# A conv and gate kernel in two layers: when the neural-CA loads are asked for, the row length of their scratch, and the order of the sync queue

## The chip, the cores and the metric

The kernel runs on one core of a Trainium2 chip. The metric is the device time of one execution in microseconds (us). Three runs of the kernel before gave 13310.97, 13316.33 and 13325.59 us; their median, 13316.33 us, is the time before.

## What is computed

The input is 32 images of 8 channels and 256 x 256 pixels. Layer 0 works on the group-normalised image and adds its result to the image; layer 1 normalises that sum and adds a quantised 3 x 3 convolution of it. The change touches layer 0 only:

```python
xn = gn(x)
grid = drive = xn                                   # "lattice" (CML)
for _ in range(15):
    mapped = 3.9 * grid * (1.0 - grid)
    physics = 0.7 * mapped + 0.3 * conv3x3_per_channel(mapped, K_local)
    grid = 0.85 * physics + 0.15 * drive
cml = clip(grid, 0.0001, 0.9999)
nca = sigmoid(conv1x1(relu(conv3x3(xn, Wp) + bp), Wu) + bu)      # 8 -> 128 -> 8 channels
gin = concat([xn, cml, nca])                         # 24 channels
g = sigmoid(conv1x1(relu(conv3x3(gin, Wg1) + bg1), Wg2) + bg2)
out0 = x + g * cml + (1 - g) * nca
```

## The kernel before

Everything that the stages of layer 0 hand on to each other goes through scratch in DRAM. `gs_s` holds three planes of an image: the normalised input, the lattice's result and the NCA's result. `xp_s` holds the normalised input once more, split in a high and a low part for the NCA's matmuls, as `[268 rows, 2 parts, 8 channels, 258 columns]`: a row has a zero column at either end, so that a 3 x 3 window can slide over it. `y_s` holds what layer 1 reads.

Five pieces of work are written into one program for TensorE (PE):

- **prep** (`normalise`, from L293): for an image and a channel pair it loads `xr`, takes the statistics (VectorE, and two tiny matmuls), normalises in place, and makes `xq` (ScalarE, L366), `hi` (VectorE, L372) and `lo` (POOL, L373). `hi` and `lo` are tiles of 258 columns of which 256 are written. `stores` (L332, L342) sends them to `gs_s` and `xp_s`.
- **lattice** (L392): a unit is one channel of four images; there are 64 units. A unit runs 15 steps of two halves `s`, so there are 1920 halves. A half is 32 matmul instructions from L499 and three `mark` matmuls (L274), which read one of the formats `m_a` or `m_b`; VectorE then adds the drive (L510) and writes the mapped grid into the other format (L520). Every half that ends in `m_a`, except in a unit's last step, is followed by `exchange` (L474, L475): two DMAs of 33 KB from SBUF to SBUF that copy border rows between neighbouring strips. There are 896 such pairs. The `m_a` that they complete is read by the next half of the same `s`, two halves later. From step 7 on the drives of the next unit are loaded (`d_a`, then `d_b` from `d_a`), and after the last step the results are stored: `background` (L462) issues four of these small DMAs after each half.
- **nca** (L576): an image has eight tiles `t` of 32 rows. A tile is loaded into `im` by the four DMAs of `rows` (L561, the DMA is L566; two buffers). It is worked through in four pieces `i` of two `hidden` calls each (12 matmuls from L585 and a ReLU on ScalarE, L593) and a `drain` (eight matmuls, L601). The result of a tile is stored at L632, in the third piece of the tile after it.
- **gate** (L705): an image has eight tiles. `stage` (L656) loads a tile's `gin` by six DMAs (L663; two buffers for each) and `mix` by two (L672; one buffer). The 240 matmul instructions of L759 make the hidden layer, those of L715 the gate. What VectorE, ScalarE and POOL do afterwards is cut into `chores`: `mix_`, `arrange_`, `stage_`, `measured_`, `extremes_`. One chore is taken from the list at each lattice half. `arrange_` (L685 to L689) reads `mix`; `extremes_` ends in the store to `y_s` (L735).
- **layer 1** (from L911), after all of this.

`together` (L844) interleaves them by hand: after each lattice half it advances a mixture of nca, gate and prep until that has done its share by the weights that the `yield`s carry (an nca tile has 14.8 in all: 1.4 for each `hidden`, 0.9 for each `drain`).

`manual_schedule(engines={PE})` at L258 says that PE's instructions keep the order in which the program writes them. Those of the other engines, and of the sync queue (SP), which issues nearly all DMAs, are put in order by the scheduler of the compiler, by its own reckoning of when each will be ready. A DMA that has to wait for its data stands at the head of its queue meanwhile: SP stood 3264.7 us in all at L474, in 800 waits, until VectorE had written `m_a`.

In `nca` the next tile is asked for in the third piece, after both of its `hidden` calls:

```python
if i == 2:
    if done:
        nc.sync.dma_start(*done)
        done = None
    if t < NT8 - 1:
        ahead = rows(b, t + 1)
```

Of the kernel before, what the change touches and what calls it, by code (L numbers as in the profile page):

```python
# [31 lines left out]
F32 = mybir.dt.float32  # L32
# [8 lines left out]
P = 128  # L41
# [9 lines left out]
STEP = 14  # L51
PW = W + 2
PROWS = 268
ROW = 2 * C * PW
PART = PROWS * C * W
R4 = 32
NT = 9
# [52 lines left out]
def kernel(  # L110
# [48 lines left out]

    xp_s = [dp.tile([PROWS, 2, C, PW], F32, name=f"xp_s{i}") for i in range(NBUF)]
    gs_s = [dp.tile([3, PROWS, C, W], F32, name=f"gs_s{i}") for i in range(NBUF)]
    y_s = [dp.tile([PROWS, C, W], F32, name=f"y_s{b}") for b in range(B)]

    with tc.tile_pool(name="prep", bufs=1) as pp, tc.tile_pool(name="prep2", bufs=2) as pp2:
# [21 lines left out]
        G.memset(zt, 0.0)  # L188
        borders = []
        for t, at, n, w, rows in (  # L190
            *((t, 0, 2 * C, PW, ((0, 1), (257, 1))) for t in xp_s),
            *((t, j * PART, C, W, ((0, 1), (257, 1))) for t in gs_s for j in range(3)),
            *((t, 0, C, W, ((0, 1), (257, 5), (262, 5), (267, 1))) for t in y_s),
        ):
            k = 64 if w == W else 43
# [59 lines left out]
    with ExitStack() as one:  # L255


        one.enter_context(tc.manual_schedule(engines={mybir.EngineType.PE}))  # L258

        pool = lambda name, bufs, **kw: one.enter_context(  # L260
            tc.tile_pool(name=name, bufs=bufs, reuse_waits="tile", **kw)
        )
        hp, xp, sp2, gp, gip = pool("hp", 4), pool("xp", 3), pool("sp2", 1), pool("gp", 3), pool("gip", 2)
        st, imp, wk, np_ = pool("st", 2), pool("imp", 2), pool("wk", 2), pool("np", 1)
        ps_u, ps_a, ps_m = pool("ps_u", 3, space=PSUM), pool("ps_a", 1, space=PSUM), pool("ps_m", 1, space=PSUM)
        LOW, HIGH = slice(0, 64), slice(64, P)

# [6 lines left out]
            T.matmul(one_[HIGH], qw[HIGH, 0, HIGH], qw[HIGH, 0, 0:1], start=True, stop=True)  # L274

        fixed = lambda shape, name, dt=F32: np_.tile(shape, dt, name=name)
        hi, lo = fixed([P, 2, 2, PW], "hi", F32R), fixed([P, 2, 2, PW], "lo", F32R)
        for t in (hi, lo):
            for w in (0, PW - 1):
                G.memset(t[:, :, :, w].bitcast(F32), 0.0)  # L280
        TU = 2 * NT
# [11 lines left out]
        def normalise(jobs):  # L293
# [36 lines left out]
            def stores(b, g, xq):  # L330
                for h in range(2):
                    nc.sync.dma_start(  # L332
                        dram_ap(
                            gs_s[b % NBUF],
                            ((1 + P * h) * C + 2 * g) * W,
                            [[C * W, P], [W, 2], [1, W]],
                        ),
                        xq[:, :, h].rearrange("p c q j -> p c (q j)"),
                    )
                for h in range(2):  # L340
                    for j, src in enumerate((hi, lo)):
                        nc.sync.dma_start(  # L342
                            dram_ap(
                                xp_s[b % NBUF],
                                (1 + P * h) * ROW + (C * j + 2 * g) * PW,
                                [[ROW, P], [PW, 2], [1, PW]],
                            ),
                            src.bitcast(F32)[:, :, h, :],
                        )
                ready.add((b, g))  # L350

            def end(b, gs, xrs, e):
                n = len(gs)
                pv = unit()[:, 0, :]
                T.matmul(pv[:, 0:n], avg, e, start=True, stop=True)
                rstd = rstd_x[:, b, gs[0] : gs[0] + n]
                V.tensor_scalar(rstd, pv[:, 0:n], GN_EPS, None, ALU.add)
                G.tensor_tensor(rstd, rstd, mhalf[:, 0:n], ALU.pow)
                for g, xr in zip(gs, xrs):
                    flat = xr.rearrange("p c h w -> p (c h w)")  # L360
                    V.tensor_scalar(
                        flat, flat, mean_x[:, b, g : g + 1], rstd_x[:, b, g : g + 1],
                        ALU.subtract, ALU.mult,
                    )
                    xq = sp2.tile([P, 2, 2, 4, NJ], F32, name="xq", tag="xq")
                    S.activation(  # L366
                        xq.rearrange("p c h q j -> p (c h) q j"),
                        xr.rearrange("p c h (j q) -> p (c h) q j", q=4),
                        AF.Copy,
                    )  # L370
                    inner = lambda t: t[:, :, :, 1 : 1 + W]
                    V.tensor_copy(inner(hi), xr)  # L372
                    G.tensor_tensor(inner(lo), xr, inner(hi).bitcast(F32), ALU.subtract)  # L373
                    yield 0.05
                    stores(b, g, xq)
                    yield 0.05
# [15 lines left out]
        def lattice(g):  # L392
# [76 lines left out]
            def exchange(t):  # L469
# [4 lines left out]
                nc.sync.dma_start(t[0::16, :, below], t[14::16, :, above])  # L474
                nc.sync.dma_start(t[15::16, :, above], t[1::16, :, below])  # L475

            JOBS = ((0, 5), (5, 10), (10, 14), (14, 18))
            HALVES = ((slice(0, 10), 5), (slice(10, 18), 4))

            def half(c, step, s, d, m_a, m_b):  # L480
# [42 lines left out]
                if a2b:  # L523
                    edge = m_b[:, :, 0 : NJ + 1 : NJ]
                    G.tensor_tensor(edge, edge, junk.unsqueeze(1).to_broadcast([P, TU, 2]), ALU.mult)  # L525
                else:
                    exchange(m_a)
                return a2b

            if g == 0:  # L530
# [5 lines left out]
            for c in range(C):  # L536
                u = g * C + c
                for step in range(STEPS):
                    if step == 7 and u + 1 < NG * C:
                        units[u + 1], dmas = load(u + 1)  # L540
                        later.extend(dmas)
                    if step == STEPS - 1:
                        background(len(later))
                    for s in range(2):
                        d = units[u][s][1 if (step + s) % 2 == 0 else 0]
                        a2b = half(c, step, s, d, m_a[s], m_b[s])
                        if step == STEPS - 1:
# [5 lines left out]
                        yield 2.05  # L553

            stored[g] = issued[0] + len(later)
            if g == NG - 1:
                background(len(later))
# [2 lines left out]

        def rows(b, t):  # L561

            im = imp.tile([P, 2, 8, PW], F32R, name="im", tag="im")
            for k in range(2):
                for q in range(2):
                    nc.sync.dma_start(  # L566
                        im.bitcast(F32)[64 * q : 64 * q + 48, k],
                        dram_ap(
                            xp_s[b % NBUF], (32 * t + 16 * k + 8 * q) * ROW, [[PW, 48], [ROW, 8], [1, PW]]
                        ),  # L570
                    )
            return im
# [3 lines left out]
        def nca(b):  # L576
# [45 lines left out]
            for t in range(NT8):  # L622
                im = ahead
                acc = ps_a.tile([P, 512], F32, name="acc", tag="acc")
                for i in range(4):
                    hs = {}
                    for n in (i, i + 4):
                        hs[n], hs[n + 8] = hidden([im[64 * q : 64 * q + 48, :, n, :] for q in range(2)])
                        yield 1.4
                    if i == 2:  # L630
                        if done:
                            nc.sync.dma_start(*done)  # L632
                            done = None
                        if t < NT8 - 1:
                            ahead = rows(b, t + 1)
                        elif all((b + 1, g) in ready for g in range(4)):
                            loaded[b + 1] = rows(b + 1, 0)
                    if pend:
                        done = drain() or done
                    pend = (acc, t, i, hs)  # L640
# [12 lines left out]
            V.reciprocal(sc[:, 2:3], sc[:, 1:2])  # L653
            return sc

        def stage(b, t):  # L656

            src = gs_s[b % NBUF]
            gin = []
            for j in range(3):  # L660
                t_ = gip.tile([P, 4, W], F32, name=f"gin{j}", tag=f"gin{j}")
                for h in range(2):
# [4 lines left out]
                        ),  # L667
                    )
                gin.append(t_)
            mix = gip.tile([P, 3, 2, W], F32, name="mix", tag="mix", bufs=1)  # L670
            for k in range(2):
                nc.sync.dma_start(  # L672
                    mix[:, :, k, :],
                    dram_ap(src, (32 * t + 16 * k + 1) * C * W, [[W, P], [PART, 3], [1, W]]),
                )
            return gin, mix

        flat = lambda t: t.rearrange("p k w -> p (k w)")

# [12 lines left out]
        staged = {}  # L692

        def begin_gate(b):
            return scales(b), stage(b, 0)

        PARTS = (
            (1, slice(0, 256), slice(0, 256)),
# [6 lines left out]
        def gate(b):  # L705
# [39 lines left out]
            for t in range(NT8 + 1):  # L745
# [30 lines left out]
                def arrange_(now):  # L776
                    now["df"] = arrange(sc, now["mix"])

                def stage_(now):
                    if now["t"] < NT8 - 1:  # L780
                        now["ahead"] = stage(b, now["t"] + 1)
                    elif (b + 1) % GB:
                        staged[b + 1] = begin_gate(b + 1)

                def measured_(now):
                    measured(now["was"]["t"], now["was"]["y"])
# [16 lines left out]
                while t < NT8 - 1 and "ahead" not in now and chores:  # L803
                    chores.pop(0)()
                ahead = now.get("ahead")
            while chores:
# [270 lines left out]
```

## Time and profile before

| what | value |
|---|---|
| median of three runs | 13316.33 us |
| the profiled execution | 13288.75 us |
| its span, first to last instruction | 13287.0 us |
| PE busy | 11179.9 us, 84% |
| VectorE, ScalarE, POOL busy | 7782.5, 3789.6, 1552.4 us |
| mean granted TensorE clock | 0.913 |
| DMA moved | 1769.32 MB, mean 133 GB/s |
| packets of the sync and the ScalarE queue's DMAs | 58.7% and 2.2% of 16 engines' span |

The profile names each group of instructions by its line in the kernel, its engine and the tiles that it writes and reads. "Idle before" is the time that an engine stood still just before an instruction, put down to what released it. A window of the profile gives the busy time of each engine in that stretch, with the granted share of TensorE's clock (PEclk) and the share of time in which the 16 DMA engines were busy.

### The profile page before, as it was taken

What the parts mean: (1) busy time and instruction counts of PE and PEld (TensorE: products, weight loads), DVE (VectorE), ACT (ScalarE), POOL (GpSimd) and SP (SyncE); (2) the same over time, 40 slices, a digit from 0 to 9 for tenths busy, and PEclk for the clock granted to TensorE, in tenths of its full rate; (3) what the DMA queues carried; (4) which work ended last, traced back from release to release, by engine and by line L of the source; (5) the groups of instructions that cost most, each with busy time, mean ns of one, the idle gap of its engine ahead of it and who ended that gap; (6) DMA issues with size and microseconds to landing.
All of it is one profiled execution on the core that took longest, in us unless ns stands there. A gap on an engine that the chain in (4) does not pass through costs nothing. (4 is left out here: it accounts for less than half of the span.)

```text
span 13287.0 us, 372338 instructions
## 1 busy us (share of the span) xinstructions
PE 11179.9 (84%) x165152; PEld 6938.4 (52%) x165152; DVE 7782.5 (59%) x11376; ACT 3789.6 (29%) x4034; POOL 1552.4 (12%) x2242
## 2 busy tenths in 40 slices
PE   4888888888888888888888888888888989889754
PEld 2555555555555555555555555555555555555532
DVE  4555555555555565555555556555655655556477
ACT  2222222222222222222222222222222222222233
POOL 1000011111111111111111111111111110001200
PEclk7999999999999999999999999999999999999877
DMA  6554566565666656665665666656666565555778
GB/s 164 94 102 95 102 134 129 123 132 127 135 127 130 134 128 126 130 136 122 132 132 123 134 135 130 127 127 132 128 132 133 127 127 116 113 109 123 179 242 257
DMA packets 2486569, 1769.32 MB, mean 133 GB/s; under 512 B 1034336, under 2 KB 2456032, under 8 KB 2484832
## 3 DMA queue, kind: packets, MB, share of 16 engines
q1 hardware_dynamic: 2392416, 1655.96, 58.7%
q10 hardware_dynamic: 92544, 89.54, 2.2%
q8 instruction: 1299, 21.28, 0.7%
q14 instruction: 310, 2.54, 0.1%
HBM read 1133.84 MB, written 474.94 MB: 121 GB/s over the span
## 5 line engine op out<-in xcount | busy, mean ns | idle before, releaser
L593 ACT ACTIVATE h<-pt,bp_sb 128x1024 f32<-128x1024 f32 x2048 | 2273.9, 1112 | 5982.6 <-PE pt L585 5978.3
L585 PE MATMUL pt<-im,wp_hi 48*128 48x512 f32 x12288 | 2869.3, 440 | 942.8 <-DMA im<-xp_s 769.3
L510 DVE SCALAR_TENSOR_TENSOR gt<-pt,d_b 128x650 f32<-128x650 f32 (+1 forms) x1920 | 1463.8, 763 | 2432.7 <-PE mark L274 1389.4
L499 PE MATMUL pt<-m_a,lw 64*64 64x325 f32 (+1 forms) x30720 | 2464.9, 439 | 354.9 <-DMA m_a<-m_a 223.6
L585 PE MATMUL pt<-im,wp_lo 48*128 48x512 f32 x12288 | 2660.7, 410 | 0.0
L510 DVE SCALAR_TENSOR_TENSOR gt<-pt,d_a 128x640 f32<-128x640 f32 (+1 forms) x1920 | 1446.8, 754 | 2013.6 <-PE mark L274 1059.9
L585 PEld LDWEIGHTS pt<-im,wp_hi 48*128 48x128 f32 x12288 | 1340.5, 194 | 2096.5 <-issue 1460.1
L499 PE MATMUL pt<-m_b,lw 64*64 64x256 f32 (+1 forms) x30720 | 2360.9, 425 | 67.6 <-DVE gt L510 38.1
L499 PEld LDWEIGHTS pt<-m_a,lw 64*64 64x64 f32 x30720 | 1462.2, 140 | 1185.8 <-issue 455.8
L499 PEld LDWEIGHTS pt<-m_b,lw 64*64 64x64 f32 x30720 | 1413.5, 136 | 881.8 <-issue 457.2
L759 PE MATMUL pt<-gin,gw 48*32 48x192 f32 (+2 forms) x61440 | 1321.0, 305 | 240.4 <-issue 228.7
L759 PEld LDWEIGHTS pt<-gin,gw 48*32 48x32 f32 x61440 | 1150.2, 109 | 588.8 <-issue 367.9
L585 PEld LDWEIGHTS pt<-im,wp_lo 48*128 48x128 f32 x12288 | 1345.7, 195 | 208.0
L520 DVE SCALAR_TENSOR_TENSOR m_a<-gt 128x640 f32<-128x640 f32 (+1 forms) x1792 | 1414.3, 789 | 58.5
L520 DVE SCALAR_TENSOR_TENSOR m_b<-gt 128x650 f32<-128x650 f32 (+1 forms) x1792 | 1385.7, 774 | 103.0 <-DVE gt L510 3.7
L525 POOL TENSOR_TENSOR m_b<-m_b,junk 128x36 f32<-128x36 f32 x896 | 241.9, 270 | 8498.1 <-DVE m_b L520 5232.4
L601 PE MATMUL acc<-h,wu_z 128*32 128x512 f32 x8192 | 1106.6, 611 | 0.0
L274 PE MATMUL mark<-qw 64*64 64x1 bf16 x5760 | 953.0, 165 | 3.2 <-issue 1.9
L687 POOL TENSOR_TENSOR d<-mix 128x256 f32<-128x256 f32 x512 | 554.7, 1101 | 1580.5 <-DVE gate L723 1146.5
L274 PEld LDWEIGHTS <-qw 64*64 64x64 bf16 x5760 | 642.8, 112 | 142.1 <-issue 10.3
L986 PE MATMUL pt<-qt,qw 128*128 128x512 bf16 (+1 forms) x864 | 235.0, 434 | 238.4 <-ACT ob L991 238.4
L685 ACT ACTIVATE f<-mix,sc 128x512 f32<-128x512 f32 x256 | 208.5, 815 | 679.5 <-DVE y L724 476.4
(109 smaller groups left out, 5445.8 us busy)
## 6 DMA issues: line engine op xcount, KB each, us to landing
im<-xp_s SPq DMA_DIRECT2D x1024, 387.0 KB
gin<-gs_s SPq DMA_DIRECT2D x1536, 192.0 KB
mix<-gs_s SPq DMA_DIRECT2D x512, 384.0 KB
d_a<-gs_s SPq DMA_DIRECT2D x2048, 36.0 KB
yb<-y_s ACTq DMA_DIRECT2D x28, 2432.0 KB
xp_s<-hi SPq DMA_DIRECT2D x256, 258.0 KB
xp_s<-lo SPq DMA_DIRECT2D x256, 258.0 KB
xr<-in_x_dram SPq DMA_DIRECT2D x128, 512.0 KB
```

The lines of the kernel that those rows point to most:

```text
L274: T.matmul(one_[HIGH], qw[HIGH, 0, HIGH], qw[HIGH, 0, 0:1], start=True, stop=True)
L499: T.matmul(pt[dst], lw[src, c, w, dst], rhs[src], start=first, stop=not first)
L510: V.scalar_tensor_tensor(gt.rearrange("p (u c) -> p u c", u=2), pt[:, :, : w * n], FLOOR, d[:, ts, :].rearrange("p (u t) j -> p u (t j)", ...
L520: V.scalar_tensor_tensor(to, gt, 1.0, gt, ALU.subtract, ALU.mult)
L525: G.tensor_tensor(edge, edge, junk.unsqueeze(1).to_broadcast([P, TU, 2]), ALU.mult)
L585: T.matmul(ph[:, i, :].rearrange("p (h w) -> p h w", w=W), w[64 * i : 64 * i + 48, dx, :], rhs[:, :, dx : dx + W], start=(dx == 0 and w is ...
L593: S.activation(h.rearrange("p i c -> p (i c)"), ph.rearrange("p i c -> p (i c)"), AF.Relu, bias=bp_sb)
L601: T.matmul(acc[32 * g : 32 * g + 32], wu_z[:, 24 - 8 * i : 56 - 8 * i], hs[4 * g + i], start=(i == 0), stop=(i == 3),)
L685: S.activation(f, flat(mix[:, 0]), AF.Identity, bias=sc[:, 0:1], scale=sc[:, 2:3])
L687: G.tensor_tensor(d[:, cols], mix[:, 1, k], mix[:, 2, k], ALU.subtract)
L759: T.matmul(pa[32 * i : 32 * i + 32, h, to], gw[64 * h : 64 * h + 48, j, dx, :], gin[j][64 * h : 64 * h + 48, i, of], start=(j == 0 and n = ...
L986: T.matmul(pt[:, i:j, :], w[:, dx, :], qt[b % 2][h][:, k0 + i : k0 + j, dx : dx + W], start=(dx == 0), stop=(dx == 2),)
```

## The change

Four things are done; no arithmetic on the data changes, and the number of DMAs stays the same.

1. `xp_s`, `hi` and `lo` lose their two border columns: a row is 256 columns, 1024 bytes, in place of 258. The zero columns now stand in two fixed tiles `ims` in SBUF, set once; `rows` writes the 256 columns between them.
2. `rows` for the next tile is asked for after the first `hidden` of a tile, in place of after both of the third piece.
3. SP joins PE in `manual_schedule`: the sync queue keeps the program's order. With it `exchange` is no longer written in the half that needs it, but kept in `held` and written just before the next half, which is behind the nca, gate and prep work that follows.
4. `stage` is cut in two: `inputs_` asks for `gin` as the first of the chores, `blend_` asks for `mix` where `stage_` stood, after `arrange_`.

```diff
-ROW = 2 * C * PW
+ROW = 2 * C * W
...
-    xp_s = [dp.tile([PROWS, 2, C, PW], F32, name=f"xp_s{i}") for i in range(NBUF)]
+    xp_s = [dp.tile([PROWS, 2, C, W], F32, name=f"xp_s{i}") for i in range(NBUF)]
...
-        one.enter_context(tc.manual_schedule(engines={mybir.EngineType.PE}))
+        one.enter_context(tc.manual_schedule(engines={mybir.EngineType.PE, mybir.EngineType.SP}))
...
-        hi, lo = fixed([P, 2, 2, PW], "hi", F32R), fixed([P, 2, 2, PW], "lo", F32R)
-        for t in (hi, lo):
+        hi, lo = fixed([P, 2, 2, W], "hi", F32R), fixed([P, 2, 2, W], "lo", F32R)
+        ims = [fixed([P, 2, 8, PW], f"im{i}", F32R) for i in range(2)]
+        for t in ims:
             for w in (0, PW - 1):
                 G.memset(t[:, :, :, w].bitcast(F32), 0.0)
...
-                                (1 + P * h) * ROW + (C * j + 2 * g) * PW,
-                                [[ROW, P], [PW, 2], [1, PW]],
+                                (1 + P * h) * ROW + (C * j + 2 * g) * W,
+                                [[ROW, P], [W, 2], [1, W]],
...
-                    inner = lambda t: t[:, :, :, 1 : 1 + W]
-                    V.tensor_copy(inner(hi), xr)
-                    G.tensor_tensor(inner(lo), xr, inner(hi).bitcast(F32), ALU.subtract)
+                    V.tensor_copy(hi, xr)
+                    G.tensor_tensor(lo, xr, hi.bitcast(F32), ALU.subtract)
...
+            held = []
...
                 else:
-                    exchange(m_a)
+                    held.append(m_a)
                 return a2b
...
                     for s in range(2):
+                        while held:
+                            exchange(held.pop())
                         d = units[u][s][1 if (step + s) % 2 == 0 else 0]
                         a2b = half(c, step, s, d, m_a[s], m_b[s])
...
-            im = imp.tile([P, 2, 8, PW], F32R, name="im", tag="im")
+            im = ims[(NT8 * b + t) % 2]
             for k in range(2):
                 for q in range(2):
                     nc.sync.dma_start(
-                        im.bitcast(F32)[64 * q : 64 * q + 48, k],
+                        im.bitcast(F32)[64 * q : 64 * q + 48, k, :, 1 : 1 + W],
                         dram_ap(
-                            xp_s[b % NBUF], (32 * t + 16 * k + 8 * q) * ROW, [[PW, 48], [ROW, 8], [1, PW]]
+                            xp_s[b % NBUF], (32 * t + 16 * k + 8 * q) * ROW, [[W, 48], [ROW, 8], [1, W]]
                         ),
                     )
...
                         hs[n], hs[n + 8] = hidden([im[64 * q : 64 * q + 48, :, n, :] for q in range(2)])
+                        if n == 0:
+                            if t < NT8 - 1:
+                                ahead = rows(b, t + 1)
+                            elif all((b + 1, g) in ready for g in range(4)):
+                                loaded[b + 1] = rows(b + 1, 0)
                         yield 1.4
-                    if i == 2:
-                        if done:
-                            nc.sync.dma_start(*done)
-                            done = None
-                        if t < NT8 - 1:
-                            ahead = rows(b, t + 1)
-                        elif all((b + 1, g) in ready for g in range(4)):
-                            loaded[b + 1] = rows(b + 1, 0)
+                    if i == 2 and done:
+                        nc.sync.dma_start(*done)
+                        done = None
...
-                def stage_(now):
+                def inputs_(now):
                     if now["t"] < NT8 - 1:
-                        now["ahead"] = stage(b, now["t"] + 1)
+                        now["ahead"] = [inputs(b, now["t"] + 1)]
                     elif (b + 1) % GB:
-                        staged[b + 1] = begin_gate(b + 1)
+                        staged[b + 1] = [inputs(b + 1, 0)]
+
+                def blend_(now):
+                    if now["t"] < NT8 - 1:
+                        now["ahead"].append(blend(b, now["t"] + 1))
+                    elif (b + 1) % GB:
+                        staged[b + 1] = scales(b + 1), (*staged[b + 1], blend(b + 1, 0))
...
                 steps = []
+                if t < NT8:
+                    steps.append(inputs_)
                 if last:
                     steps.append(mix_)
                 if t < NT8:
-                    steps += [arrange_, stage_]
+                    steps += [arrange_, blend_]
                 if last:
                     steps += [measured_, extremes_]
```

`inputs` and `blend` are the two parts of `stage`: the loop of six `gin` DMAs, and that of two `mix` DMAs.

More of the change, by code (lines that the diff above doesn't have):

```diff
@@ L190 @@
         for t, at, n, w, rows in (
-            *((t, 0, 2 * C, PW, ((0, 1), (257, 1))) for t in xp_s),
+            *((t, 0, 2 * C, W, ((0, 1), (257, 1))) for t in xp_s),
             *((t, j * PART, C, W, ((0, 1), (257, 1))) for t in gs_s for j in range(3)),
@@ L194 @@
         ):
-            k = 64 if w == W else 43
+            k = 64
             for row, m in rows:
@@ L263 @@
         hp, xp, sp2, gp, gip = pool("hp", 4), pool("xp", 3), pool("sp2", 1), pool("gp", 3), pool("gip", 2)
-        st, imp, wk, np_ = pool("st", 2), pool("imp", 2), pool("wk", 2), pool("np", 1)
+        st, wk, np_ = pool("st", 2), pool("wk", 2), pool("np", 1)
         ps_u, ps_a, ps_m = pool("ps_u", 3, space=PSUM), pool("ps_a", 1, space=PSUM), pool("ps_m", 1, space=PSUM)
@@ L553, in lattice @@
                         yield 2.05
+            while held:
+                exchange(held.pop())
             stored[g] = issued[0] + len(later)
@@ L654, in scales, with inputs @@
             return sc
-        def stage(b, t):
+        def inputs(b, t):
             src = gs_s[b % NBUF]
@@ L669, in stage, with blend @@
                 gin.append(t_)
+            return gin
+        def blend(b, t):
+            src = gs_s[b % NBUF]
             mix = gip.tile([P, 3, 2, W], F32, name="mix", tag="mix", bufs=1)
@@ L675, in stage @@
                 )
-            return gin, mix
+            return mix
         flat = lambda t: t.rearrange("p k w -> p (k w)")
@@ L694, in begin_gate @@
         def begin_gate(b):
-            return scales(b), stage(b, 0)
+            return scales(b), (inputs(b, 0), blend(b, 0))
         PARTS = (
@@ L802, in gate @@
                 yield 2.3 if t < NT8 else 0.9
-                while t < NT8 - 1 and "ahead" not in now and chores:
+                while t < NT8 - 1 and len(now.get("ahead", ())) < 2 and chores:
                     chores.pop(0)()
```

## The prediction

> **What bounds the kernel.** I read the page's engine rows first, then PE's waits in the long middle stage, then one stall with its windows, then what the sync queue did before it.
>
> ```profile
> PE 11179.9 (84%) x165152; PEld 6938.4 (52%) x165152; DVE 7782.5 (59%) x11376; ACT 3789.6 (29%) x4034; POOL 1552.4 (12%) x2242
> ...
> PEclk7999999999999999999999999999999999999877
> ```
>
> PE is the bound: no other engine is over 59%. Its program order is fixed by hand, so each of its idle microseconds adds to the time. Of 13287 us it is idle in 2107. Its waits between 330 and 12300 us (who waits for whom; total, times, longest):
>
> ```profile
> PE pt L585 <- DMA im<-xp_s: 744.6, 164, 13.5
> PE pt L499 <- DMA m_a<-m_a: 221.4, 79, 13.0
> PE pt L759 <- issue: 163.0, 171, 4.1
> PE pt L585 <- ACT h L593: 103.9, 87, 2.7
> PE pt L499 <- DVE gt L510: 73.3, 65, 5.8
> ```
>
> Half of all the waiting is for the NCA's tile `im`, 164 times for 256 tiles. One of them by windows (us, busy time of PE, PEld, DVE, ACT, POOL, PEclk, DMA share, GB/s):
>
> ```profile
> 7125.00:7135.60 10.60, 10.59 (x118) 5.74 (x114) 7.57 (x16) 3.34 (x3) 0.00 (x0) 1.00 0.56 131
> 7135.60:7148.00 12.40, 0.00 (x0) 0.03 (x1) 1.62 (x3) 0.00 (x0) 0.25 (x1) 0.62 1.13 208
> 7148.00:7155.60 7.60, 5.57 (x29) 3.39 (x33) 0.00 (x0) 1.11 (x1) 0.00 (x0) 0.50 1.14 160
> 7155.60:7170.00 14.40, 13.27 (x329) 8.79 (x324) 9.64 (x13) 5.35 (x7) 3.86 (x5) 1.00 0.25 56
> ```
>
> PE does nothing for 12.4 us, and for 7.6 us more it works at a clock of 0.50. The sync queue, a little earlier:
>
> ```profile
> 7129.25 2.86 SPq L663 DMA_DIRECT2D gin<-gs_s  x6
> 7132.22 1.79 SPq L672 DMA_DIRECT2D mix<-gs_s  x2
> 7134.11 0.44 SPq L632 DMA_DIRECT2D gs_s<-nca  x1
> 7134.60 3.32 SPq L566 DMA_DIRECT2D im<-xp_s  x4
> 7138.02 0.62 SPq L474 DMA_DIRECT2D m_a<-m_a  x1
> ```
>
> `im` was asked for at 7134.6, when PE was one microsecond from needing it, and behind 1.9 MB of `gin` and `mix`; with its own 1.5 MB it was usable at about 7150.7. Over all tiles, the fourth `im` DMA is issued a median of 17.0 us ahead of the tile's first matmul, and 9.0 us or less in a quarter of them. The request is late; the transfers are not too slow for the stage (DMA share 0.60).
>
> **Two rules of the Trainium skill.** "TensorE: Matmul & The Clock Gate", Part 1, says that a monitor halves PE's clock after an idle window of about 3.4 us, until PE has been busy for about as long. The windows above agree: 0.62 during the gap, 0.50 after it, 1.00 from 7155.6. So a wait costs more than its own length. "DMA: Bandwidth & Descriptors", section "How a descriptor splits into AXI transactions", says that a piece whose start isn't a multiple of 256 B needs more bus transactions than its length suggests. The packets agree as far as they can: those of 1032 B took 94.5 ns in the mean (524,288 of them), those of 1024 B 59.6 ns (809,984). In the few us after their issue `im` packets had a median of 112 ns, `gin` packets, also 48 partitions read from DRAM, 67 ns. I go by the trace for both.
>
> **The change, part by part.** The sum is made against the span, 13287.0 us; the profiled execution (13288.75) is 27.6 us under the median of the runs shown.
>
> *The earlier request.* It moves from 10.2 to 1.4 of a tile's 14.8 weights, and a tile lasts 47.6 us (median), so some 28 us are won, more where the scheduler had let it slip. The buffer allows it: tile t+1 overwrites tile t-1, whose last matmul lies before the new place. To see what the new queue order does I wrote down all SP instructions in program order with the change and laid them along the old trace: each starts when the queue is free and its producer has ended in the trace, and lasts as long as its kind did (0.4 to 0.65 us). The fourth `im` DMA then stands 33 us or more ahead of its use in 99% of tiles, with a median of 48, against a landing of some 8 to 16. So the wait goes: -740, keeping the first tile's, which has no tile ahead of it. In 28 us, some four halves, the four DMAs move past about two pairs of `exchange`, up to 17 background DMAs, a set of `gin` and `mix` and an `nca` store; that is priced below.
>
> *The clock.* By the trace's clock records 1833 us between 300 and 12700 were at half clock, in 208 stretches, and PE was busy in 1204 of them. The 12 `hidden` matmuls of L585 take 1.66 us at full and 3.2 to 5.9 at half clock, a lattice half 2.4 and 4.5, so half of the 1204, some 600 us, is loss. 115 stretches with 1191 us follow a gap at L585, 39 with 304 us one at `m_a`. The first group goes: 600 x 1191/1833 = -390. It can't be kept, unless other gaps take their place.
>
> *Rows of 1024 B.* 393,216 `im` packets and 131,072 to `xp_s`. If `im` falls from 94.5 to `gin`'s 67 ns, 393216 x 27.5 ns / 16 = 0.68 ms of each DMA engine go, out of 8.2 ms. PE does not wait for bandwidth, so directly this is 0; it shortens what an `exchange` finds ahead of it. The new pitch in SBUF (1032 B, starting 4 B in) is not shown by any load of the trace; `d_b<-d_a`, whose 256 B pieces are written at a pitch of 260 B, has the same median packet, 18 ns, as the aligned `d_a`. Bounds: 47 ns (the fastest) to 112 (nothing won). I take 67.
>
> *The queue in program order, and `exchange` behind the fill.* Now, SP stands waiting when VectorE finishes `m_a`: in 75% of cases the DMA goes out within 0.07 us, in 95% within 2.3. Laid along the trace, the new order gives 0.06 in 75% and 1.5 in 95%, since SP mostly gets through the fill's DMAs before VectorE is done. Ahead of `exchange` in its queue now stand up to four background DMAs, `im`, `gin`, `mix` and the stores, and behind their waits all SP work: 813 us of waits for the last step's clamp (L517), 169 for POOL's `f`, 126 for `y`, 135 for `d_a`. They fit: some 11,700 DMAs of about 0.55 us over 1920 halves are 3.4 us in a half of 6.4. What does not vanish is what is in the DMA rings ahead of it: an `exchange` takes 2.3 us from issue to its last packet (median), 10.1 at the 95th percentile. From issue to need there are 5.5 us (median), 4.1 in a quarter. `im`, `gin` and the stores of `prep` now come at the program's places, some just ahead of an `exchange`, and PE loses the slack that its `im` waits gave. Counting what the rings hold, wait by wait, I get 180 us with `im` packets at 47 ns, 360 at 67, 1190 at 112. Pairs behind the same load share a wait, and lost slack adds: I take 350 for 221 today, +130, and in proportion to its clock stretches (about 100 now) +60.
>
> *`gin` ahead of `mix_` and `arrange_`.* Six DMAs of 0.45 us move ahead of one or two halves' background DMAs (some 2 us each) and of one `exchange`. PE waits 11 us for `gin` today, all after 12300: 0, -10 to +10. `blend_` stays behind POOL's last read of the single `mix` buffer, so the last 430 us, where gate runs alone, keep their loop.
>
> *Small things*: two memsets of 129 ns more or fewer; `hi` (0.69 us) and `lo` (2.2 us) read without the gap, 128 each, off PE's path: 0. In the first 330 us stores can hold up the next image's load: -20 to +20, taken as 0. VectorE, ScalarE and POOL are still ordered by the scheduler and may come out differently, and with less idling PE will meet them more often (waits at `h`, `gt`, `rstd` of some 250 us now): +30.
>
> Sum: 13287 - 740 - 390 + 130 + 60 + 30 = 12377; with what lies around the span and the distance to the median (+29) 12406. I say 12420.
>
> **The rivals.**
>
> 1. *`exchange` is no later than now* (0.20). For it: smaller `im` packets, and SP that waits at `exchange` anyway. Then 12377 - 190 leaves 12187, with the 29 some 12200; if its waits shrink too, 12080.
> 2. *The rings* (0.17). If the SBUF side makes the packets dear (95 ns), `exchange` waits 790 us: +570, +200 of clock in place of 190: 12990, or 12900 with shared waits. Against it: the fast `d_b` packets.
> 3. *The queue blocks* (0.06): slower. The place is L474. In program order a store whose producer VectorE or POOL is late with stands ahead of `exchange`. There are 5.5 - 2.3 = 3.2 us to spare; all of the 1130 us gained are gone when 896 exchanges make PE wait 1.26 us each, that is from a mean lateness of about 4.5 us. At 5 us: 896 x 1.8 = 1610, so 13800. Against it: the 1.5 us above, and that SP would have to be late at every one.
> 4. *It does not do what it says* (0.03): the request is written early, but SP gets there late, and the wait stays: 13300.
>
> The forecast has 0.54, and its own range is 12200 to 12700. The range of 8 in 10 leaves out cases 3 and 4, half of 2 and the far end of 1: 12080 to 12920. Within 0.2% of 13316 (what a measurement can tell) only case 4 ends, 0.03; slower is case 3, 0.06; faster is the rest, 0.91.
>
> **What would show it.** Right: the row `pt L585 <- DMA im<-xp_s` falls under 60 us, and PEclk stands at 0.96 or more in the middle; no 1032 B packets; SP still waits for VectorE at `exchange`. The `m_a` row shows the new price: 150 to 600. Wrong would be an `im` row of some hundreds (case 4), an `m_a` row over 800 with DMA queued ahead (2), or with `exchange` issued late (3), or long waits for VectorE at L499.

## The result and the profile after

The changed kernel took 13370.76 us (median of 5; 13350.67 to 13379.49) against 13316.33 (median of 5): ratio 1.0036, 95% interval 1.0021 to 1.0051. It is slightly slower, where 12420 was forecast. The profiled execution has a span of 13348.8 us, 61.8 more than before.

The page's engine row and clock row hardly differ from those before:

```profile
PE 11191.9 (84%) x165152; PEld 6958.4 (52%) x165152; DVE 7851.3 (59%) x11376; ACT 3786.3 (28%) x4034; POOL 1574.7 (12%) x2242
...
PEclk7999999999999999999999999999999999999877
```

PE's waits between 330 and 12300 us do differ (L500, L590, L769 are what L499, L585, L759 were):

```profile
PE pt L769 <- issue: 638.2, 211, 8.8
PE pt L500 <- DMA m_a<-m_a: 549.5, 138, 10.5
PE pt L590 <- ACT h L598: 105.0, 83, 2.0
PE pt L500 <- DVE gt L511: 65.3, 80, 2.1
```

`im` is not among the long waits any more. Over the whole span the three rows were, before:

```profile
PE pt L585 <- DMA im<-xp_s: 769.3, 166, 22.6
PE pt L759 <- issue: 228.7, 208, 4.4
PE pt L499 <- DMA m_a<-m_a: 223.6, 81, 13.0
```

and are, with the change:

```profile
PE pt L769 <- issue: 709.8, 250, 8.8
PE pt L500 <- DMA m_a<-m_a: 559.7, 144, 10.5
PE pt L590 <- DMA im<-xp_s: 19.9, 2, 18.2
```

Two rows have grown in place of `im`: the gate's matmuls waiting for "issue", and the exchange. The three differences, -749.4, +481.1 and +336.1, add up to +67.8 us, and the span grew by 61.8 (PE's busy time by 12.0). So the gain was made in full and given back.

"Issue" is time in which PE waits for nothing that the profile shows. What it waits for is seen in one gate tile of the changed kernel, first by the sync queue, then by PE:

```profile
6667.53 1.93 SPq L571 DMA_DIRECT2D im<-xp_s  x4
6675.44 0.62 SPq L474 DMA_DIRECT2D m_a<-m_a  x1
6676.11 0.62 SPq L475 DMA_DIRECT2D m_a<-m_a  x1
6676.77 4.31 SPq L668 DMA_DIRECT2D gin<-gs_s  x6
```

```profile
6673.78 2.63 PE L769 MATMUL pt<-gin,gw 48*32 48x256 f32 x126
6680.99 1.60 PE L769 MATMUL pt<-gin,gw 48*32 48x63 f32 x41 [4.57 <-issue]
```

and by windows (us, PE, PEld, DVE, ACT, POOL, PEclk, DMA share, GB/s):

```profile
6674.00:6676.40 2.40, 2.40 (x126) 2.16 (x110) 2.33 (x5) 0.61 (x1) 0.30 (x1) 1.00 1.15 141
6676.40:6681.00 4.60, 0.03 (x3) 0.01 (x3) 3.56 (x9) 0.81 (x1) 3.23 (x4) 0.85 1.08 175
6681.00:6685.00 4.00, 4.00 (x118) 3.73 (x122) 0.00 (x0) 0.16 (x1) 0.00 (x0) 0.50 0.87 191
```

`im` is asked for at 6667.5, the DMA engines are full (a share of 1.08 to 1.15), PE gets through about half of the gate's 240 matmuls and 240 weight loads in 2.6 us, and then stands still for 4.6 us and goes on at half clock. The page shows a DMA queue for instructions:

```profile
q8 instruction: 1298, 21.27, 0.7%
```

These are 1298 packets of 16,384 bytes. PE's 330,304 matmuls and weight loads are 254 to a packet, so nearly all of them are PE's, at 64 bytes an instruction and 256 to a packet. In the packet records one starts at 6677.49, a microsecond after PE has stopped, and has landed at 6679.25; PE goes on 1.7 us later. It is the rule: there are 171 stalls of over 1 us inside a gate; in 145 a block lands within the stall, in the others less than 1 us before it, and they end 1.25 to 1.68 us after the last block landed (5th to 95th percentile, median 1.45). Of 234 other stalls of PE over 1 us between 330 and 12000 us only 23 end 1.2 to 1.75 us after a block, against 166 of the 171. The gate uses 480 instructions, nearly two blocks, in 4.66 us when nothing stops it. The Trainium skill, "Runtime: NRT & Kernel Launch", section "Instruction fetch mechanics", says that each engine's sequencer fetches the next 16 KiB block by a DMA queue of its own and that this is mostly hidden. Block size and queue agree with the trace; hidden it was not here, where 710 us of PE were lost in front of and inside gates.

### The profile page after: what moved, and what is told of

Its sections match the earlier page's. It is cut to its first block, busy times and chain, and to the rows that moved or that the text cites. A ratio compares the mean times of both kernels' runs of the same rounds, so it can differ in the third digit from the quotient of the medians.

```text
span 13348.8 us, 372548 instructions
## 1 busy us (share of the span) xinstructions
PE 11191.9 (84%) x165152; PEld 6958.4 (52%) x165152; DVE 7851.3 (59%) x11376; ACT 3786.3 (28%) x4034; POOL 1574.7 (12%) x2242
## 3 DMA queue, kind: packets, MB, share of 16 engines
q8 instruction: 1298, 21.27, 0.7%
## 5 line engine op out<-in xcount | busy, mean ns | idle before, releaser
L500 PE MATMUL pt<-m_a,lw 64*64 64x260 f32 (+1 forms) x30720 | 2528.3, 449 | 641.1 <-DMA m_a<-m_a 559.7
L590 PE MATMUL pt<-im,wp_hi 48*128 48x512 f32 x12288 | 2632.3, 425 | 152.0 <-ACT h L598 106.8
L500 PE MATMUL pt<-m_b,lw 64*64 64x320 f32 (+1 forms) x30720 | 2433.5, 436 | 123.9 <-DVE gt L511 61.3
L590 PE MATMUL pt<-im,wp_lo 48*128 48x512 f32 x12288 | 2442.6, 394 | 0.7 <-issue 0.7
L500 PEld LDWEIGHTS pt<-m_a,lw 64*64 64x64 f32 x30720 | 1525.8, 143 | 1470.2 <-issue 794.7
L769 PE MATMUL pt<-gin,gw 48*32 48x192 f32 (+2 forms) x61440 | 1422.0, 321 | 753.1 <-issue 709.8
L500 PEld LDWEIGHTS pt<-m_b,lw 64*64 64x64 f32 x30720 | 1444.8, 140 | 957.3 <-issue 529.7
L590 PEld LDWEIGHTS pt<-im,wp_hi 48*128 48x128 f32 x12288 | 1163.3, 186 | 1274.3 <-issue 768.9
L769 PEld LDWEIGHTS pt<-gin,gw 48*32 48x32 f32 x61440 | 1218.2, 115 | 1137.5 <-issue 872.6
L590 PEld LDWEIGHTS pt<-im,wp_lo 48*128 48x128 f32 x12288 | 1169.2, 186 | 204.4 <-issue 0.9
L777 ACT ACTIVATE r<-pt,bv 128x512 f32<-128x512 f32 x256 | 175.8, 687 | 1181.4 <-PE pt L769 1181.3
```

The costliest lines, as they stand in the source:

```text
L500: T.matmul(pt[dst], lw[src, c, w, dst], rhs[src], start=first, stop=not first)
L590: T.matmul(ph[:, i, :].rearrange("p (h w) -> p h w", w=W), w[64 * i : 64 * i + 48, dx, :], rhs[:, :, dx : dx + W], start=(dx == 0 and w is ...
L769: T.matmul(pa[32 * i : 32 * i + 32, h, to], gw[64 * h : 64 * h + 48, j, dx, :], gin[j][64 * h : 64 * h + 48, i, of], start=(j == 0 and n = ...
L777: S.activation(r1.rearrange("p (k w) -> p k w", w=W), pa[:, :, :W], AF.Relu, bias=bv[:, 0:1])
```

## The experiments

Theory 1: where `im`'s 1.5 MB stand. Moved to the first piece, they are in the DMA rings (DMAs that the queue has issued and that are not yet carried out) just when the gate needs instruction blocks, and ahead of exchanges. Theory 2: slack. A PE that doesn't wait for `im` outruns its instruction fetch and its exchange wherever `im` is asked for. Theory 3: the sync queue's program order makes the exchange late.

Ratios are to runs of the kernel before made beside each kernel, whose medians lay between 13284 and 13316 us, with their 95% intervals; kernels are compared by these ratios. Waits are PE's over the whole span of the profiled execution. An exchange can come late in two ways: *lateness* is the time from VectorE's end to its first DMA's issue; what it takes from issue to its last packet beyond the usual 2.3 us is put down to the *ring*. Each wait for `m_a` is counted under the larger of the two.

| kernel | time, us | ratio | `im` wait | gate's issue | `m_a` wait |
|---|---|---|---|---|---|
| before | 13316 | 1 | 769 | 229 | 224 |
| changed | 13371 | 1.0036 (1.0021 to 1.0051) | 20 | 710 | 560 |
| a_ask_late | 13806 | 1.0376 (1.0359 to 1.0394) | 296 | 217 | 1164 |
| a_ask_n2 | 12836 | 0.9650 (0.9631 to 0.9670) | 21 | 213 | 744 |
| a_spread | 12565 | 0.9441 (0.9422 to 0.9460) | 21 | 393 | 328 |
| a_im_eighth | 12004 | 0.9020 (0.9003 to 0.9037) | 11 | 217 | 163 |
| b_early | 13117 | 0.9875 (0.9853 to 0.9898) | 24 | 746 | 308 |
| b_rows | 13257 | 0.9976 (0.9967 to 0.9985) | 738 | 225 | 212 |
| a_sched_sp | 13036 | 0.9818 (0.9793 to 0.9843) | 20 | 714 | 311 |
| a_gin_late | 13484 | 1.0157 (1.0134 to 1.0180) | 21 | 625 | 823 |
| no_held | 13475 | 1.0147 (1.0127 to 1.0166) | 21 | 782 | 623 |
| align | 13275 | 0.9978 (0.9969 to 0.9987) | 20 | 674 | 543 |
| s_sched | 12404 | 0.9326 (0.9307 to 0.9346) | 20 | 421 | 170 |
| s_later | 12489 | 0.9396 (0.9377 to 0.9416) | 21 | 242 | 430 |
| s_gin | 12578 | 0.9457 (0.9429 to 0.9485) | 21 | 345 | 389 |
| s_later_sched | 12445 | 0.9375 (0.9358 to 0.9393) | 61 | 311 | 288 |

**a_ask_late**: the request back in the third piece, the rest as changed.

```diff
-                        if n == 0:
-                            if t < NT8 - 1:
-                                ahead = rows(b, t + 1)
...
+                    if i == 2:
...
+                        if t < NT8 - 1:
+                            ahead = rows(b, t + 1)
```

> The changed kernel with one part undone: a tile's im is asked for in the third piece again, as before the change. Theory 1 (the load's place): in the first piece its 1.5 MB stand in the DMA rings while the gate's matmuls run, so PE's instruction blocks and the exchange behind it come late. Then L769's idle by issue falls from 710 to about 200 us and m_a's from 560 to about 250, the im wait comes back with 300 to 700, and the time is 13100 to 13350. Theory 2 (no slack: a PE that no longer waits for im outruns its instruction fetch and its exchange wherever im is asked for): the same rows, since PE waits for im again; this run can't tell 1 from 2. Theory 3 (the sync queue's program order makes the exchange late): m_a stays over 500.

Issue fell to 217 as theory 1 says, but the time was missed by 450 us: `m_a` rose to 1164. Of this, 1091 us are waits in which the ring was the larger part of the delay, not a late issue, and in 1047 of them `im` had been asked for in the 9 us before the exchange. From issue to last packet the exchanges that PE waited for took 5.5 us more than the usual 2.3 on average. In program order this place puts the burst just ahead of exchanges.

**a_ask_n2**: asked for after the first `hidden` of the third piece, after the last place where a gate can begin.

```diff
-                        if n == 0:
+                        if n == 2:
```

> The changed kernel with im asked for after the first hidden of the third piece (n == 2): by the program's order the gate's matmuls always begin at one of the first five hiddens of a tile, so here they are past. Theory 1 (the load's place): the im wait stays under 150 us, L769's issue goes to about 250 and m_a to about 300: 12750. Theory 2 (no slack): issue stays over 600 and m_a over 500: about 13300. Theory 3 (the queue's order): m_a stays over 500: about 12950.

```profile
PE pt L500 <- DMA m_a<-m_a: 744.2, 212, 11.4
...
PE pt L769 <- issue: 212.5, 202, 4.7
```

No wait for `im` beyond the first tile's, and issue at 213: PE does not outrun its instruction fetch when no burst stands beside the gate. For the fetch theory 2 falls. For the exchange this run can't refute it: `m_a` went up and not down, as theories 2 and 3 say, so the time gained is smaller than theory 1 gave. Lateness was the larger part in 471 of the 744 us, which speaks for theory 3; that slack alone doesn't make the exchange wait is shown by a_im_eighth and s_sched below, with no wait for `im` either and `m_a` at 163 and 170.

**a_spread**: the same request cut in four, one DMA after each of the first four hiddens.

```diff
-                        if n == 0:
+                        if n in (0, 4, 1, 5):
+                            if n == 0:
+                                later_im = []
                                 if t < NT8 - 1:
-                                    ahead = rows(b, t + 1)
+                                    ahead, later_im = rows(b, t + 1)
...
+                            if later_im:
+                                nc.sync.dma_start(*later_im.pop(0))
```

> The changed kernel with the four DMAs of im written one by one after the first four hiddens of a tile in place of all four after the first. The same bytes, at about the same place, but never more than one DMA (0.4 MB) in the rings ahead of an instruction block or an exchange. Theory 1, if it is the burst that hurts: issue about 350, m_a about 300: 12750. Theory 1, if the bytes near the gate hurt in any case: issue about 600. Theory 2 (no slack): issue over 600, m_a over 500: about 13300.

```profile
PE pt L777 <- issue: 393.3, 229, 6.5
PE pt L500 <- DMA m_a<-m_a: 328.2, 152, 7.7
```

The same bytes, asked for from the same place on, and 12565 us in place of 13371. It is mostly the burst that hurts; issue still stands 165 us over the kernel before. Gates with two or more `im` DMAs issued between 8 us before their start and their end lose 5.5 us each to gaps in the changed kernel (90 gates), 2.5 here (89 gates), and the others 1.3 and 1.0.

**a_im_eighth**: one row in place of eight in each of the four DMAs.

```diff
-                        im.bitcast(F32)[64 * q : 64 * q + 48, k, :, 1 : 1 + W],
+                        im.bitcast(F32)[64 * q : 64 * q + 48, k, 0:1, 1 : 1 + W],
```

> The changed kernel with one of eight rows in each of im's DMAs: as many DMAs at the same places, an eighth of the bytes. It leaves out seven eighths of the NCA's input, which stay zero. Theory 1 (the load in the rings): L769's issue falls under 150 us and m_a under 150: about 12250. Theory 2 (no slack): PE waits for im no more than in the changed kernel, so issue stays over 600 and m_a over 500: about 13300. Theory 3 (the queue's order): m_a stays over 500.

```profile
PE pt L768 <- issue: 216.7, 212, 3.9
PE pt L499 <- DMA m_a<-m_a: 163.1, 104, 4.5
```

It leaves out seven eighths of the NCA's input, so it is no version of the kernel. The bytes, not the number of the DMAs and not their place alone, carry both costs: 217 and 163 us are left, and a gate beside an `im` request loses 0.8 us, like the others (0.9). Issue did not fall under 150 as expected: 213 to 229 us of it are also there in the kernel before, b_rows, a_ask_late and a_ask_n2, where `im` is asked for late in the tile. What causes these is not shown.

**b_early**: the kernel before with the earlier request alone.

> The kernel before with only the earlier request: im asked for after the first hidden, rows of 258 columns, sync queue left to the scheduler. If the load's place is what costs (theory 1), the im wait goes (under 100 us) and L759's issue rises from 230 to 500 to 800, with m_a at 300 to 600: 13100 to 13400, about what the whole change gives. If the sync queue's program order is what takes the gain back (theory 3), issue and m_a stay near 230 and 224: about 12500.

```profile
PE pt L760 <- issue: 746.2, 259, 8.3
PE pt L499 <- DMA m_a<-m_a: 307.6, 106, 13.3
```

The moved request alone brings the issue stalls; nothing else in the change is needed for them. `m_a` grew by 84 only, where the changed kernel has +336: the next run shows that the rest belongs to the queue's order. The request alone is a gain of 1.25%.

**a_sched_sp**: the changed kernel, sync queue given back to the scheduler.

```diff
-manual_schedule(engines={mybir.EngineType.PE, mybir.EngineType.SP})
+manual_schedule(engines={mybir.EngineType.PE})
...
-                    held.append(m_a)
+                    exchange(m_a)
```

> The changed kernel with the sync queue given back to the scheduler and the exchange written in the half, as before. Theory 1 (the load's place, whatever the order): L769's issue stays at 500 to 800, m_a at 400 to 700: 13200 to 13500. Theory 3 (the order takes the gain back): m_a near 224 and exchanges out within 0.1 us of VectorE in 75% of cases: under 12900.

```profile
PE pt L769 <- issue: 714.2, 260, 9.3
PE pt L500 <- DMA m_a<-m_a: 311.2, 113, 12.8
```

Issue stays at 714, `m_a` falls from 560 to 311: theory 3 holds for the exchange, theory 1 for the gate. The program's order, with the exchange held back, costs 2.2% here (0.9818 against 1.0036). Exchanges go out within 0.07 us of VectorE in 75% of cases and 1.5 in 95%; in the changed kernel within 1.5 and 7.9.

**b_rows**: the kernel before with rows of 256 columns alone.

> The kernel before with only the rows of 256 columns (and the two fixed tiles that hold im's zero columns). Packets of im counted 1032 bytes and 94.5 ns; in the changed kernel those of 1024 bytes have a mean of 73.4 ns over all loads, which leaves about 94.7 for im: no gain. Expected from that: im wait within 50 us of the 769 of before and the time within 0.5% of it. If the aligned rows did help the load, the im wait falls by 100 or more.

A gain of 0.24%, by a shorter `im` wait; the mean over all packets of 1024 B is 71.9 ns, which leaves about 91 for those of `im` and `xp_s` (94.5 before) if the others keep their 59.6.

**a_gin_late**: `gin` asked for again with `mix`.

```diff
-                if t < NT8:
-                    steps.append(inputs_)
...
-                    steps += [arrange_, blend_]
+                    steps += [arrange_, lambda now: (inputs_(now), blend_(now))]
```

> The changed kernel with gin asked for where stage_ stood, just ahead of mix, after arrange_: two lattice halves later. If gin's 1.2 MB near the gate delay the instruction blocks beside im, L769's issue falls from 710 to 400 to 550 and the time by 100 to 250. If im alone does it (gates with im issued beside them lost 5.5 us each in the changed kernel, those with gin alone 1.2), issue stays over 600 and the time within 0.7% of the changed kernel's 13370.

Issue fell by 85 only and stayed over 600, so `im` is what matters there. But `m_a` rose by 264, and the time by 1.2%, which was not expected: asking for `gin` first pays in this order of the queue, through the exchange.

**no_held**: program order, the exchange written in its half.

```diff
-                    held.append(m_a)
+                    exchange(m_a)
```

> The changed kernel, sync queue in program order, with each exchange written in its half again, so that the queue stands at it until VectorE is done and all DMAs of the fill that follows come after it. If it is the fill's DMAs written ahead of the exchange that make it late (1.5 us or more in a quarter of cases, 7.9 in one of twenty), lateness goes to the scheduler's 0.1 in 75% and m_a from 560 to about 310, the figure under the scheduler: about 13050. If holding it back was right, the DMAs behind it are held up instead, and m_a or other waits rise: 13400 or more.

Lateness fell (0.4 us in 75%, 4.1 in 95%; its mean from 1.45 to 0.66), so holding the exchange back made part of it. Yet `m_a` rose to 623 and issue to 782: the waits moved to the ring, 609 of the 623 us, 559 of them with `im` asked for in the 9 us before. In this order of the queue holding the exchange back was right, by 1.1%.

**align**: `im` at a pitch of 288 columns, its data from column 16.

```diff
-        ims = [fixed([P, 2, 8, PW], f"im{i}", F32R) for i in range(2)]
+        ims = [fixed([P, 2, 8, 288], f"im{i}", F32R) for i in range(2)]
...
-                        im.bitcast(F32)[64 * q : 64 * q + 48, k, :, 1 : 1 + W],
+                        im.bitcast(F32)[64 * q : 64 * q + 48, k, :, 16 : 16 + W],
```

> The changed kernel with im's rows at a pitch of 288 columns in SBUF and the data from column 16, so that each row of 1024 bytes starts at a multiple of 64 in SBUF as it does in gin's tiles (before: 1032 bytes apart, from byte 4). If the address in SBUF is why im's packets did not get cheaper, their mean falls and that of all 1024-byte packets goes from 73.4 ns to about 62, and with the shorter burst L769's issue and m_a fall by a third: about 13000. If the burst itself (four DMAs queued on 16 engines) makes them slow, the mean stays within 3 ns and the time within 0.5% of 13370.

0.6% faster than the changed kernel, with a packet mean of 71.8 ns (73.4 there): at most a small effect of the address, not the cause of slow packets.

**s_sched**: a_spread with the scheduler's sync queue.

> im's four DMAs spread over a tile's first four hiddens, with the sync queue given back to the scheduler and the exchange written in the half. With the burst ahead, the program's order cost 13370 - 13036 = 334 us (m_a 560 against 311). If the order costs by itself, this run is 100 to 300 under the spread one in program order (12565). If it only cost because the burst stood ahead of the exchange, the two are within 100 us.

```profile
PE pt L777 <- issue: 421.0, 227, 6.9
...
PE pt L500 <- DMA m_a<-m_a: 169.8, 103, 5.5
```

12404 us, 6.7% under the kernel before and the fastest full version. The order costs 1.2% even without the burst; `m_a` fell by 158 us, under what it was in the kernel before, and issue rose by 28.

**s_later**: a_spread over the third to sixth hidden.

```diff
-                        if n in (0, 4, 1, 5):
+                        if n in (1, 5, 2, 6):
```

> im's four DMAs spread over the third to the sixth hidden of a tile in place of the first four, sync queue in program order. The gate begins within the first five hiddens, so fewer bytes of im are in the rings beside it: L777's issue from 393 to 250 to 300. The last DMA is asked for some 20 us ahead of its use, one at a time, against a landing of 3 to 5: im wait under 50. About 12450; over 12565 if m_a rises instead.

Issue fell by 151 to 242, as expected; `m_a` rose by 101.

**s_gin**: a_spread with two of `gin`'s six DMAs in each of three chores.

> The spread kernel with gin spread too: two of the six DMAs with each of three chores in place of all six with the first. If gin's 1.2 MB at once also hold up instruction blocks and exchanges, issue falls from 393 to about 320 and m_a from 328 to about 270: about 12450. If only im mattered, within 60 us of 12565.

Issue fell by 48 and `m_a` rose by 60; the interval overlaps a_spread's. It gains nothing.

**s_later_sched**: the later places of s_later with the scheduler's sync queue of s_sched.

> im spread over the third to the sixth hidden, sync queue given to the scheduler, exchange in the half. If the two gains are of different things (the instruction blocks beside the gate: issue 393 to 242 by the later place; the exchange: m_a 328 to 170 by the scheduler's order), they add: about 12330. If the scheduler moves the requests about so that the later place is lost, or the lead gets too short (im wait over 50), 12400 or more.

They do not add: the fourth `im` DMA is issued less than 6 us ahead of its use in a tenth of the tiles, `im` waits return with 61 us and `m_a` is at 288. s_sched stays the best.

## Why the prediction was wrong

The span came out 972 us over the forecast's 12377. Of this the gate's issue is 481, the clock 342 (its terms came to -330, and PE's busy time rose by 12), the exchange 206, and all else -57.

*The earlier request* was right in itself: -740 forecast, -749 measured. The fourth `im` DMA stands 35 us or more ahead of its use in 99% of tiles (33 forecast), with a median of 43.5 (48).

*The step that failed* is the end of that paragraph: "the four DMAs move past about two pairs of `exchange`, up to 17 background DMAs, a set of `gin` and `mix` and an `nca` store; that is priced below". It listed the queue's instructions that the request moves past, but not what PE does at the new place. The gate's row, `L759 <- issue`, stood third in the list of waits and was put at no change without a reason. It is PE's own instruction stream, which comes by DMA too, and it grew by 481 us. The phase can be read from the program and the traces: a gate begins at one of the first five hiddens of a tile (all but the last 34 of 256 gates, which come when the NCA is done), so the old place, after the sixth, was out of its way and the new one is not. Gates with two or more `im` DMAs beside them were 16 before and 90 after. None of the rivals had this, and none of the signs named to tell right from wrong looked at it: `im` fell under 60 and `m_a` lay between 150 and 600, as for a forecast that holds, and only the clock's sign failed. a_ask_n2, b_early and a_im_eighth show the step.

*The exchange* was right in kind and too small: 350 forecast, 560 measured. Of the 560, the ring was the larger part of the delay in 427 us of waits (208 before) and lateness in 132 (16 before). Two terms were too small. The packets of `im` were taken at 67 ns and stayed at about 95 (1,334,272 packets of 1024 B have a mean of 73.4; those that were of 1024 B before, 59.6). That is the packet time of rival 2, which gave 790 us for the exchange: the packet time came true, and that price was too high. And laying the new order along the old trace gave a lateness of 1.5 us at the 95th percentile, where 7.9 was measured; the mean is 1.45, far from the 4.5 of rival 3. The layout let each DMA be issued in 0.4 to 0.65 us. Of 896 exchanges 252 went out over 1 us late, 1229 us in all, and for 475 of these SP stood in waits put down to `im`'s DMAs, also at instructions that read nothing of `im`. This is taken for full rings; the trace does not name them. At the exchange itself such waits were 54 us before and 301 after. Under the scheduler (a_sched_sp) 1.5 us is what came out, but for another order.

*The clock*, -390, failed with it. The forecast's own condition was "unless other gaps take their place": 1284 us of PE's work still ran at half clock (1204 before), 134 stretches with 980 us after a gap in the gate and 89 with 632 after one at `m_a`. That a long gap costs again at half clock holds for the new gaps too. (In the stall that the prediction shows, PE worked 5.6 of the 7.6 us at half clock; for 2.0 us of them it still waited for `im`.)

*Rows of 1024 B* at 0 directly: b_rows gained 0.24%; most of the saving in packet time did not come, so the rule on unaligned starts of the Trainium skill, "DMA: Bandwidth & Descriptors", section "How a descriptor splits into AXI transactions", can't be read from packet times here. *`gin` ahead*: forecast 0; without it the changed kernel is 1.2% slower. *Small things* are not told apart.

With the burst spread and nothing else changed, the kernel runs in 12565 us, within the forecast's own range. This does not bear out the sum: `im` (-749) and the exchange (+105) come out near it, but the gate's issue still adds 165, and PE's busy time falls by 169 where the clock was put at -330.

What stays open: why `im`'s packets take about 90 ns where others take 60. Neither the length of the row, nor the address in SBUF, nor the burst (a_spread: 70.8 over all, so about 88) explains more than a few. Nor do the packet records show what holds an instruction block up, its turn at a DMA engine or something ahead of that; they show that it starts late, and later when `im`'s bytes are near.

## What to carry to other kernels

Before a large load is moved to an earlier place, look at what runs at that place and needs a transfer at once: a wait that is gone because 1.5 MB come sooner can return as a wait for a small transfer behind them. A long run of short matmuls is such a place, since its own instructions come by DMA. Idle time put down to "issue" inside such a run needs a term of its own in the sum. Ask early, but in pieces: in this kernel four DMAs of 0.4 MB, one after each of four `hidden` calls, kept most of the gain that one burst gave back.

## What the runs showed of the hardware

- In the changed kernel instruction blocks of 16,384 bytes take 0.9 to 1.9 us in their packet records (1st to 99th percentile), with a mean of 1.27 near a gate and 1.20 elsewhere; inside a gate PE goes on about 1.45 us after one has landed.
- The loss is in when a block starts. No fetch in the body of these traces starts before PE has begun 149 instructions more than a multiple of 256. Counted from the 150th, the fetches that start inside a gate do so after a median of 1.7 us in the kernel before and in a_im_eighth, 4.0 in the changed kernel and 4.9 in b_early.
- A gate of 480 PE instructions takes 4.66 us undisturbed, and 11.49 or more in a quarter of cases in the changed kernel (clock included).
- In the changed kernel an exchange, two DMAs of 33 KB, takes 2.3 us from issue to its last packet in the median and up to 14.9.
